# A four-layer graph kernel: LSTM input kept graph by graph, and layer 3's weights multiplied together on the chip

## The chip, the cores and the metric

The kernel runs on one core of a Trainium2 chip. The metric is the device time of one execution in microseconds (us). All data are float32.

## The reference

The input x is 128 graphs x 64 nodes x 256 features, 8192 tokens in all. Four layers each add something to x after a layernorm and a relu. Cut to what matters:

```
# layer 0: two graph convolutions, then LSTMs over windows of p = 1..4 nodes
h = relu(adj @ (h @ Wg0 + bg0)); h = relu(adj @ (h @ Wg1 + bg1))
for p in 1..4:                       # nw = 64 // p windows per graph
    wins = h[:, :nw*p].reshape(B*nw, p, 256)
    last = lstm_last(Wih[p-1], Whh[p-1], ..., wins)
    h[:, arange(nw)*p + (p-1)] = last        # the last node of each window is replaced
# layer 1: A_hat @ x, linear 256->512, batchnorm, relu, linear 512->256, batchnorm
# layer 2: three weights, with the diagonal, upper and lower part of adj, and a bias
# layer 3: causal attention inside each graph, with adj added to the scores
q, k, v = split(h @ Wqkv)
attn = softmax(where(causal, q @ k.T * scale + adj, -1e30))
y = (attn @ v) @ Wo
```

## The kernel before, in words

Tokens are handled in 16 supertiles of 512 (`NS`, `SUP`), two graphs per 128 partitions, or with features on partitions and tokens along the row (`KC` = 2 chunks of 128 features). One list of Python loops writes the program; the tile framework adds the waits and may hoist an instruction, but each engine runs its own instructions in order. Every matmul writes one of eight PSUM banks (`bank()`, all under the name `ps`). Loads of tokens and LSTM weights are issued on SP's queue, loads of constants on ScalarE's.

The stages are:

- **Layer 0, first part** (lines 206 to 232): for each supertile, layernorm, two aggregations and two linear maps. The last line, L232, applies the relu and writes the features into `hT`.
- **LSTM** (lines 235 to 307): for p = 1 to 4, weights `wih` and `whh` are loaded and the tokens are taken in blocks of up to 512 windows, two blocks at a time. `step` makes the gates: for each gate half, two products of `wih` with node j of each window, read from `hT` by `cols`, and from the second node on two of `whh` with the state `hn` (all L276), then an activation (L278). VectorE combines the gates (L285 to L294), and L298 writes the last state back into `hT`. When j = 0 the forget gate is left out, so a block has 12 products with `wih` for the first node and 16 for each later one.
- **Layer 1** (lines 324 to 379): a first pass over the supertiles makes the token-major x1 (transposes at L185), aggregates, multiplies with `w1` (L350) and gathers statistics; a second pass (L366 to L378) follows when all statistics are in.
- **Layers 2 and 3** (lines 382 to 476): for each supertile, transposes back, layernorm (L158 to L165), aggregation (L400), layer 2's products (L411), layernorm, transposes of h (L421) into `h3T` (L422), products with `wqkv` for q and k (L427, copied by ScalarE at L429), for v (L435, L438), scores (L443), softmax (L446 to L453), transposes of the weights (L456, L458), the product with v (L463, L465), with `wo` (L470), and the sum (L473), which is stored. Every supertile is written out in this order, and its steps depend on each other.

A group of `hT` holds 2048 tokens, 32 graphs. Node t of graph b lies at column t x 32 + b, so for any p and j `cols` reads runs of 32 adjacent words. Because layer 1 wants the tokens of one graph together, GpSimd copies each supertile's features into `hs` first (L341, through `graphs`). There is one group of memory more than groups of tokens (`hbuf`, the last in the pool `hlast`), since `place(s)` lets layer 1's results lie one group behind their inputs. The pool `late` takes hlast's place when layer 1's first pass is over, and only then are layer 2's and layer 3's weights loaded (L357 to L360), which the trace has at 1657.7 to 1661.2 us.

Of the kernel before, what the change touches and what calls it, by code (L numbers as in the profile page):

```python
# [20 lines left out]
def kernel(ctx: ExitStack, tc: tile.TileContext, a: dict, out: bass.AP):  # L21
# [37 lines left out]

    def load_const(name, src, shape, pool=const):  # L60
        t = pool.tile(shape, F32, tag=name, name=name)
        nc.scalar.dma_start(t, src)
        return t

    def row_bcast(name, src, n, pool=const):
        t = pool.tile([P, n], F32, tag=name, name=name)
        nc.scalar.dma_start(t, bass.AP(tensor=src.tensor, offset=src.offset, ap=[[0, P], [1, n]]))
        return t

    def weight(name, src, pool=const):  # L70
        k, m = src.shape
        return load_const(name, src.rearrange("(c p) m -> p c m", p=P), [P, k // P, m], pool)

# [24 lines left out]
    bn1 = load_const("bn1", a["bn1"], [P, 3, HC])  # L98
    bn2 = load_const("bn2", a["bn2"], [P, 3, KC])

    lbias = const.tile([P, NL, NM], F32, tag="lbias", name="lbias")
# [77 lines left out]
    def to_token_major(src, add, dst):  # L179

        for q2 in range(0, Q, 2):
# [5 lines left out]

    last = ExitStack()  # L190
    hlast = last.enter_context(tc.tile_pool(name="hlast", bufs=1, side="right"))
    hbuf = [(hpool if g < NG else hlast).tile([P, KC, GRP], F32, tag=f"hT{g}", name=f"hT{g}")
            for g in range(NG + 1)]
    hT = hbuf[1:]

    def place(s):
        return hbuf[s // SG], (s % SG) * SUP

    def graphs(s, c):

        v = hT[s // SG][:, c, :].rearrange("p (t b) -> p b t", b=GB)
        b = (s % SG) * (SUP // T)
        return v[:, b : b + SUP // T, :]


    with tc.tile_pool(name="pa", bufs=2) as pa, tc.tile_pool(name="pax", bufs=3) as pax:
        for s in range(NS):
            xt = pax.tile([P, Q, D], F32, tag="xt", name="xt")
            nc.sync.dma_start(xt, x_r[s])
            h = layernorm_relu(pa, xt)  # L210
            g0 = aggregate(pa, h, adjT_bd, "g0")
            h1 = pa.tile([P, Q, D], F32, tag="h1", name="h1")
            for q2 in range(0, Q, 2):
                p_ = bank().rearrange("p (q d) -> p q d", q=2)
                for q in range(2):
                    for c in range(KC):
                        nc.tensor.matmul(p_[:, q, :], g0[:, c, ts(q2 + q, P)], wg0[:, c, :],
                                         start=(c == 0), stop=(c == KC - 1))
                nc.vector.tensor_add(h1[:, q2 : q2 + 2, :], p_,
                                     rsb[:, None, :].to_broadcast([P, 2, D]))  # L220
            nc.scalar.activation(h1, h1, AF.Relu)
            g1 = aggregate(pa, h1, adjT_bd, "g1")
            for o in range(KC):
                p_ = bank()
                for c in range(KC):
                    nc.tensor.matmul(p_, wg1[:, c, ts(o, P)], g1[:, c, :],
                                     start=(c == 0), stop=(c == KC - 1))
                t = pa.tile([P, SUP], F32, tag="h2", name="h2")
                nc.vector.scalar_tensor_tensor(
                    t.rearrange("p (q n) -> p q n", q=Q), bcast_q(rs_row), bg1[:, o : o + 1],  # L230
                    p_.rearrange("p (q n) -> p q n", q=Q), op0=ALU.mult, op1=ALU.add)
                nc.scalar.activation(graphs(s, o), t.rearrange("p (b t) -> p b t", t=T), AF.Relu)  # L232


    with tc.tile_pool(name="lw", bufs=2) as lw, tc.tile_pool(name="lg", bufs=2) as lg, \
            tc.tile_pool(name="lh", bufs=3) as lh:
        for p in range(1, NL + 1):
# [7 lines left out]
            nw = T // p  # L245
            per = 512 // GB
            nblk = -(-nw // per)
            cut = [i * nw // nblk for i in range(nblk + 1)]
            blocks = [(g, w0, w1 - w0) for g in range(NG) for w0, w1 in zip(cut, cut[1:])]

            def cols(blk, c, j):
                g, w0, n = blk
                v = hT[g][:, c, :].rearrange("p (t b) -> p t b", b=GB)
                return v[:, w0 * p + j : (w0 + n - 1) * p + j + 1 : p, :]

            def step(blk, j, state):
                last = j == p - 1
                N = blk[2] * GB
                gate = {}
                for name, gi, fn in (("i", 0, AF.Sigmoid), ("g", 2, AF.Tanh),  # L260
# [5 lines left out]
                    for hc in range(KC):  # L266
# [5 lines left out]
                        for n, (w, r, c) in enumerate(ops):  # L272
                            o_ = p_[:, :N]
                            if n < KC:
                                o_ = o_.rearrange("p (w b) -> p w b", b=GB)
                            nc.tensor.matmul(o_, w[:, c, ts(m, P)], r,  # L276
# [19 lines left out]
                else:  # L296
                    for c in range(KC):
                        nc.vector.tensor_mul(  # L298
                            cols(blk, c, j),
                            gate["o"][:, c, :N].rearrange("p (w b) -> p w b", b=GB),  # L300
                            gate["g"][:, c, :N].rearrange("p (w b) -> p w b", b=GB))

# [21 lines left out]

    with tc.tile_pool(name="pz", bufs=1) as pz:
        zb = [pz.tile([P, HC - KC, SUP], F32, tag=f"z{s}", name=f"z{s}") for s in range(NS)]
# [7 lines left out]

        with tc.tile_pool(name="pb", bufs=2) as pb, tc.tile_pool(name="pbx", bufs=2) as pbx:
            for s in range(NS):
                xt = pbx.tile([P, Q, D], F32, tag="xt", name="xt")
                nc.sync.dma_start(xt, x_r[s])
                hs = pb.tile([P, KC, SUP], F32, tag="hs", name="hs")
                for c in range(KC):  # L340
                    nc.gpsimd.tensor_copy(hs[:, c, :].rearrange("p (b t) -> p b t", t=T), graphs(s, c))  # L341
                x1 = pbx.tile([P, Q, D], F32, tag="x1", name="x1")
                to_token_major(lambda c, q: hs[:, c, ts(q, P)], xt, x1)
                nc.sync.dma_start(x1d[s], x1)
                h = layernorm_relu(pb, x1)
                ag = aggregate(pb, h, ahT, "ag")
                for o in range(HC):
                    p_ = bank()
                    for c in range(KC):
                        nc.tensor.matmul(p_, w1[:, c, ts(o, P)], ag[:, c, :],  # L350
                                         start=(c == 0), stop=(c == KC - 1))
                    z = zslot(s, o)
                    nc.scalar.activation(z, p_, AF.Identity, bias=bn1[:, 0, o : o + 1])
                    nc.vector.bn_stats(st1[:, o, s, :], z)
        last.close()
        late = ctx.enter_context(tc.tile_pool(name="late", bufs=1, side="right"))
        wl2 = [weight(f"wl2_{k}", a["W"][k], late) for k in range(3)]  # L357
        bl2 = row_bcast("bl2", a["bias"], D, late)
        wqkv = weight("wqkv", a["Wqkv"], late)
        wo = weight("wo", a["Wo"], late)  # L360
        co1 = bn_coeffs(pz, st1, HC, bn1, "bn1")

        for s in range(NS):
# [11 lines left out]
            for o in range(KC):  # L375
                y = zslot(s, o)
                nc.vector.tensor_scalar_add(y, acc[o], bn2[:, 0, o : o + 1])
                nc.vector.bn_stats(st2[:, o, s, :], y)  # L378
        co2 = bn_coeffs(pz, st2, KC, bn2, "bn2")


    with tc.tile_pool(name="pc", bufs=2) as pc, tc.tile_pool(name="pc1", bufs=1) as pc1:
        for s in range(NS):
# [34 lines left out]
            for c in range(KC):  # L418
# [3 lines left out]
                nc.vector.tensor_copy(h3T[:, c, :], p_)  # L422
            qk = pc1.tile([P, 2 * KC, SUP], F32, tag="qk", name="qk")
            for o in range(2 * KC):
                p_ = bank()
                for c in range(KC):
                    nc.tensor.matmul(p_, wqkv[:, c, ts(o, P)], h3T[:, c, :],  # L427
                                     start=(c == 0), stop=(c == KC - 1))
                nc.scalar.copy(qk[:, o, :], p_)  # L429
            v = pc.tile([P, Q, D], F32, tag="v", name="v")  # L430
            for q2 in range(0, Q, 2):
                p_ = bank().rearrange("p (q d) -> p q d", q=2)
                for q in range(2):
                    for c in range(KC):
                        nc.tensor.matmul(p_[:, q, :], h3T[:, c, ts(q2 + q, P)],  # L435
                                         wqkv[:, c, 2 * D : 3 * D],
                                         start=(c == 0), stop=(c == KC - 1))
                nc.scalar.copy(v[:, q2 : q2 + 2, :], p_)  # L438

            p_ = bank()  # L440
            for q in range(Q):
                for c in range(KC):
                    nc.tensor.matmul(p_[:, ts(q, P)], qk[:, c, ts(q, P)], qk[:, KC + c, ts(q, P)],  # L443
                                     start=(c == 0), stop=(c == KC - 1))
# [15 lines left out]
            for c in range(KC):  # L460
                p_ = bank()
                for q in range(Q):
                    nc.tensor.matmul(p_[:, ts(q, P)], v[:, q, ts(c, P)], eT[:, ts(q, P)],  # L463
                                     start=True, stop=True)
                nc.scalar.copy(yT[:, c, :], p_)  # L465
            for q2 in range(0, Q, 2):
                p_ = bank().rearrange("p (q d) -> p q d", q=2)
                for q in range(2):
                    for c in range(KC):
                        nc.tensor.matmul(p_[:, q, :], yT[:, c, ts(q2 + q, P)], wo[:, c, :],  # L470
                                         start=(c == 0), stop=(c == KC - 1))
# [43 lines left out]
```

## Time and profile before

| | us |
|---|---|
| median of 2 runs (2765.78 to 2766.38) | 2766.08 |
| the profiled execution | 2765.78 |
| its span, first to last instruction | 2764.1 |
| layer 0, first part, until the first LSTM matmul | 243.8 |
| LSTM p = 1, 2, 3, 4 | about 168, 308, 337, 371 |
| layer 1, first and second pass | about 280 and 118 |
| layers 2 and 3 | about 936 |

PE is TensorE's matmul, PEld its weight load, DVE VectorE, ACT ScalarE, POOL GpSimd, SP the engine that issues token loads. In the profile one float32 matmul leaves two PE records. [...] the distance from one start to the next, or busy time divided by count, says what a record takes of the stream. Groups in the tables are named by line; L165 and L185 are helpers used by several stages.

### The profile page before, as it was taken

To read this page: it belongs to the slowest core of one execution; us is meant where nothing else is said; L and a number is where in the kernel's file an instruction comes from. 1 tells how busy PE (TensorE), PEld (TensorE's weight loads), DVE (VectorE), ACT (ScalarE), POOL (GpSimd) and SP (SyncE) were. 2 spreads that over 40 slices of the span, in tenths; PEclk is the share of its full clock that TensorE was granted. 3 is DMA by queue.
4 is the path that set the end of the run, shared out by engine and by line. 5 is a ranking of instruction groups with operands and counts; after the bars stand their busy time and mean duration, and the time that the engine had idled before them with its cause. 6 is when DMAs were issued, how large, how long until landed. Compare 5 with 4: busy or idle time off the path is not lost. (4 is left out here: it accounts for less than half of the span.)

```text
span 2764.1 us, 18958 instructions
## 1 busy us (share of the span) xinstructions
PE 2398.7 (87%) x7588; PEld 1419.9 (51%) x7588; DVE 778.9 (28%) x1564; ACT 787.6 (28%) x1331; POOL 139.0 (5%) x126
## 2 busy tenths in 40 slices
PE   6888999999999999999986667978778787787877
PEld 5664444444666665444444444445555555555555
DVE  5542221112222121121124443452222222222222
ACT  3333442333333233222222224302222222222221
POOL 1000000000000000000011110000010000000000
PEclk9999999999999999999998898988888888888888
DMA  3101000000000000000001111000000000000000
GB/s 110 39 16 61 0 13 3 1 0 0 31 1 0 0 0 0 0 0 0 0 15 61 61 64 56 0 23 15 16 31 16 15 16 16 31 16 16 16 8 16
DMA packets 35977, 54.29 MB, mean 20 GB/s; under 512 B 2608, under 2 KB 29488, under 8 KB 35888
## 3 DMA queue, kind: packets, MB, share of 16 engines
q1 hardware_dynamic: 31856, 49.29, 5.5%
q10 hardware_dynamic: 4032, 3.78, 0.4%
q8 instruction: 60, 0.98, 0.2%
q14 instruction: 29, 0.24, 0.0%
HBM read 36.28 MB, written 16.78 MB: 19 GB/s over the span
## 5 line engine op out<-in xcount | busy, mean ns | idle before, releaser
L276 PE MATMUL ps<-hT,wih 128*128 128x512 f32 (+2 forms) x2016 | 810.9, 542 | 7.1 <-DMA wih<-in_WihT_dram 7.1
L276 PEld LDWEIGHTS ps<-hT,wih 128*128 128x128 f32 x2016 | 383.7, 190 | 387.5 <-issue 322.4
L276 PE MATMUL ps<-hn,whh 128*128 128x512 f32 (+2 forms) x1152 | 466.2, 527 | 0.0
L276 PEld LDWEIGHTS ps<-hn,whh 128*128 128x128 f32 x1152 | 218.9, 190 | 200.4 <-issue 153.1
L165 ACT ACTIVATE ln_h<-x,ln_rn 128x256 f32<-128x256 f32 x192 | 99.6, 589 | 523.2 <-DVE ln_rn L162 523.2
L400 PE MATMUL ps<-adj,ln_h 128*128 128x384 f32 x256 | 126.5, 667 | 84.8 <-ACT ln_h L165 84.8
L411 PE MATMUL ps<-wl,ag 128*128 128x256 f32 x768 | 168.4, 379 | 0.0
L278 ACT ACTIVATE gg<-ps,lbias 128x512 f32<-128x512 f32 (+2 forms) x144 | 91.9, 638 | 231.9 <-PE ps L276 231.9
L411 PEld LDWEIGHTS ps<-wl,ag 128*128 128x128 f32 x768 | 145.9, 190 | 23.3
L278 ACT ACTIVATE gi<-ps,lbias 128x512 f32<-128x512 f32 (+2 forms) x144 | 91.8, 638 | 229.9 <-PE ps L276 229.9
L427 PE MATMUL ps<-h3T,wqkv 128*128 128x512 f32 x256 | 144.8, 730 | 9.1 <-DVE h3T L422 9.1
L288 DVE TENSOR_TENSOR gi<-gi,gg 128x1024 f32<-128x1024 f32 (+2 forms) x36 | 38.2, 1062 | 385.6 <-ACT gg L278 385.6
L400 PEld LDWEIGHTS ps<-adj,ln_h 128*128 128x128 f32 x256 | 67.1, 270 | 138.4 <-ACT ln_h L165 88.8
L175 PE MATMUL ps<-ahT,ln_h 128*128 128x128 f32 x256 | 61.0, 429 | 86.2 <-ACT ln_h L165 86.2
L278 ACT ACTIVATE go<-ps,lbias 128x512 f32<-128x512 f32 (+2 forms) x144 | 91.3, 634 | 89.1 <-PE ps L276 86.8
L350 PE MATMUL ps<-ag,w 128*128 128x512 f32 x256 | 116.6, 605 | 0.0
L161 POOL TENSOR_TENSOR ln_rn<-ln_rn,mhalf 128x4 f32<-128x4 f32 x64 | 64.8, 1012 | 987.4 <-DVE ln_rn L160 979.2
L427 PEld LDWEIGHTS ps<-h3T,wqkv 128*128 128x128 f32 x256 | 60.0, 242 | 87.1 <-issue 63.3
L341 POOL COPY hs<-hT 128x512 f32<-128x512 f32 x32 | 32.8, 1061 | 1422.0 <-DVE hT L298 1254.8
L175 PEld LDWEIGHTS ps<-ahT,ln_h 128*128 128x128 f32 x256 | 57.5, 316 | 90.0 <-ACT ln_h L165 90.0
L285 DVE TENSOR_TENSOR cell<-gi,gg 128x1024 f32<-128x1024 f32 (+2 forms) x36 | 41.2, 1144 | 210.3 <-ACT gg L278 210.3
L291 ACT ACTIVATE gg<-cell 128x1024 f32<-128x1024 f32 (+1 forms) x72 | 68.7, 954 | 82.2 <-DVE cell L290 82.2
(121 smaller groups left out, 2265.6 us busy)
## 6 DMA issues: line engine op xcount, KB each, us to landing
xt<-in_x_dram SPq DMA_DIRECT2D x32, 512.0 KB, 4.5
x1d<-x SPq DMA_DIRECT2D x16, 512.0 KB, 2.9
x<-x1d SPq DMA_DIRECT2D x16, 512.0 KB, 3.9
out_dram<-x SPq DMA_DIRECT2D x16, 512.0 KB, 3.1
wih<-in_WihT_dram SPq DMA_DIRECT2D x4, 1024.0 KB, 5.6
whh<-in_WhhT_dram SPq DMA_DIRECT2D x3, 1024.0 KB, 9.2
wl<-in_W_dram ACTq DMA_DIRECT2D x3, 256.0 KB, 5.5
wqkv<-in_Wqkv_dram ACTq DMA_DIRECT2D x1, 768.0 KB, 7.2
```

Source lines behind the costliest of these rows:

```text
L161: nc.gpsimd.tensor_tensor(rn[:, 0, :], rn[:, 0, :], mhalf[:, :Q], ALU.pow)
L165: nc.scalar.activation(h[:, q, :], src[:, q, :], AF.Relu, bias=rn[:, 1, q : q + 1], scale=rn[:, 0, q : q + 1])
L175: nc.tensor.matmul(p_[:, ts(q, P)], h[:, q, ts(c, P)], mT, start=True, stop=True)
L276: nc.tensor.matmul(o_, w[:, c, ts(m, P)], r, start=(n == 0), stop=(n == len(ops) - 1))
L278: nc.scalar.activation(gt[:, hc, :N], p_[:, :N], fn, bias=lbias[:, l, m : m + 1])
L285: nc.vector.tensor_mul(c_, i_, g_)
L288: nc.vector.tensor_mul(i_, i_, g_)
L291: nc.scalar.activation(g_, c_, AF.Tanh)
L350: nc.tensor.matmul(p_, w1[:, c, ts(o, P)], ag[:, c, :], start=(c == 0), stop=(c == KC - 1))
L400: nc.tensor.matmul(p_, h[:, q, ts(c, P)], adj3.rearrange("p k n -> p (k n)"), start=True, stop=True)
L411: nc.tensor.matmul(p_[:, q, :], ag[:, c, k, ts(q2 + q, P)], wl2[k][:, c, :], start=(n == 0), stop=(n == 3 * KC - 1))
L427: nc.tensor.matmul(p_, wqkv[:, c, ts(o, P)], h3T[:, c, :], start=(c == 0), stop=(c == KC - 1))
```

## The change

Two things are exchanged in one diff.

*The LSTM buffer.* `hT` is laid out graph by graph: node t of graph b lies at column b x 64 + t. `cols` then reads element steps of p words, in runs of one graph's windows. L232's write and layer 1's transposes use adjacent words, so `graphs`, `hs` and the GpSimd copies are gone, and so are `hlast` and `late`. The blocks are taken over graphs: `nb` graphs with all their windows, 512 columns for p = 1, 2 and 4 and 336 for p = 3 (before: 320 and 352), and as many blocks as before (16, 8, 8, 4).

*Layer 3.* Between layer 0's first part and the LSTM a new block loads Wqkv and Wo, transposes Wq, Wk and Wv, and makes wqk = Wq Wk^T and wvo = Wv Wo once. In layer 3, `h3T` takes the place of k in the scores and the layernorm's result h the place of v; `wvo` stands for `wo`.

Besides, layer 2's weights and bias are loaded with the other constants at the start, and layer 1's pool of input tiles has three buffers instead of two.

```diff
+    wl2 = [weight(f"wl2_{k}", a["W"][k]) for k in range(3)]
+    bl2 = row_bcast("bl2", a["bias"], D)
...
-        v = hT[s // SG][:, c, :].rearrange("p (t b) -> p b t", b=GB)
...
-                nc.scalar.activation(graphs(s, o), t.rearrange("p (b t) -> p b t", t=T), AF.Relu)
+                nc.scalar.activation(dst[:, o, c0 : c0 + SUP], t, AF.Relu)
+    with tc.tile_pool(name="wt", bufs=1) as wt:
+        wqkv = wt.tile([P, KC, 3 * D], F32, tag="wqkv", name="wqkv")
+        nc.scalar.dma_start(wqkv, a["Wqkv"].rearrange("(c p) m -> p c m", p=P))
+        wo = wt.tile([P, KC, D], F32, tag="wo", name="wo")
+        nc.scalar.dma_start(wo, a["Wo"].rearrange("(c p) m -> p c m", p=P))
+        wT = wt.tile([P, 3 * KC, D], F32, tag="wT", name="wT")
+        for k in range(3):
+            p_ = bank().rearrange("p (d c) -> p d c", d=KC)
+            for d in range(KC):
+                for c in range(KC):
+                    nc.tensor.transpose(p_[:, d, ts(c, P)], wqkv[:, c, ts(k * KC + d, P)], ident)
+            nc.vector.tensor_copy(wT[:, k * KC : (k + 1) * KC, :], p_)
+        for left, right, to in ((0, wT[:, KC : 2 * KC, :], wqk), (2, wo, wvo)):
+            p_ = bank().rearrange("p (c m) -> p c m", c=KC)
+            for c in range(KC):
+                for d in range(KC):
+                    nc.tensor.matmul(p_[:, c, :], wT[:, left * KC + d, ts(c, P)], right[:, d, :],
+                                     start=(d == 0), stop=(d == KC - 1))
+            nc.vector.tensor_copy(to, p_)
...
-                g, w0, n = blk
-                v = hT[g][:, c, :].rearrange("p (t b) -> p t b", b=GB)
-                return v[:, w0 * p + j : (w0 + n - 1) * p + j + 1 : p, :]
+                g, b = blk
+                v = hT[g][:, c, :].rearrange("p (b t) -> p b t", t=T)
+                return v[:, b : b + nb, j : j + (nw - 1) * p + 1 : p]
...
-                hs = pb.tile([P, KC, SUP], F32, tag="hs", name="hs")
-                for c in range(KC):
-                    nc.gpsimd.tensor_copy(hs[:, c, :].rearrange("p (b t) -> p b t", t=T), graphs(s, c))
...
-            qk = pc1.tile([P, 2 * KC, SUP], F32, tag="qk", name="qk")
-            for o in range(2 * KC):
+            qk = pc1.tile([P, KC, SUP], F32, tag="qk", name="qk")
+            for o in range(KC):
...
-                    nc.tensor.matmul(p_, wqkv[:, c, ts(o, P)], h3T[:, c, :],
+                    nc.tensor.matmul(p_, wqk[:, c, ts(o, P)], h3T[:, c, :],
...
-            v = pc.tile([P, Q, D], F32, tag="v", name="v")
-            for q2 in range(0, Q, 2):
-                p_ = bank().rearrange("p (q d) -> p q d", q=2)
...
-                    nc.tensor.matmul(p_[:, ts(q, P)], qk[:, c, ts(q, P)], qk[:, KC + c, ts(q, P)],
+                    nc.tensor.matmul(p_[:, ts(q, P)], qk[:, c, ts(q, P)], h3T[:, c, ts(q, P)],
...
-                    nc.tensor.matmul(p_[:, ts(q, P)], v[:, q, ts(c, P)], eT[:, ts(q, P)],
+                    nc.tensor.matmul(p_[:, ts(q, P)], h[:, q, ts(c, P)], eT[:, ts(q, P)],
...
-                        nc.tensor.matmul(p_[:, q, :], yT[:, c, ts(q2 + q, P)], wo[:, c, :],
+                        nc.tensor.matmul(p_[:, q, :], yT[:, c, ts(q2 + q, P)], wvo[:, c, :],
```

More of the change, by code (lines that the diff above doesn't have):

```diff
@@ L57, in bank, with load_const, row_bcast, weight @@
         return psum.tile([P, 512], F32, tag="ps", name="ps")
-    def load_const(name, src, shape, pool=const):
-        t = pool.tile(shape, F32, tag=name, name=name)
+    def load_const(name, src, shape):
+        t = const.tile(shape, F32, tag=name, name=name)
         nc.scalar.dma_start(t, src)
         return t
-    def row_bcast(name, src, n, pool=const):
-        t = pool.tile([P, n], F32, tag=name, name=name)
+    def row_bcast(name, src, n):
+        t = const.tile([P, n], F32, tag=name, name=name)
         nc.scalar.dma_start(t, bass.AP(tensor=src.tensor, offset=src.offset, ap=[[0, P], [1, n]]))
         return t
-    def weight(name, src, pool=const):
+    def weight(name, src):
         k, m = src.shape
-        return load_const(name, src.rearrange("(c p) m -> p c m", p=P), [P, k // P, m], pool)
+        return load_const(name, src.rearrange("(c p) m -> p c m", p=P), [P, k // P, m])
     ident = const.tile([P, P], F32, tag="ident", name="ident")
@@ L99 @@
     bn2 = load_const("bn2", a["bn2"], [P, 3, KC])
+    wl2 = [weight(f"wl2_{k}", a["W"][k]) for k in range(3)]
+    bl2 = row_bcast("bl2", a["bias"], D)
+    wqk = const.tile([P, KC, D], F32, tag="wqk", name="wqk")
+    wvo = const.tile([P, KC, D], F32, tag="wvo", name="wvo")
     lbias = const.tile([P, NL, NM], F32, tag="lbias", name="lbias")
@@ L186, in to_token_major @@
             nc.vector.tensor_add(dst[:, q2 : q2 + 2, :], add[:, q2 : q2 + 2, :], p_)
[L190 to L194, printed above, removed]
-    def place(s):
-        return hbuf[s // SG], (s % SG) * SUP
-    def graphs(s, c):
-        v = hT[s // SG][:, c, :].rearrange("p (t b) -> p b t", b=GB)
-        b = (s % SG) * (SUP // T)
-        return v[:, b : b + SUP // T, :]
+    hT = [hpool.tile([P, KC, GRP], F32, tag=f"hT{g}", name=f"hT{g}") for g in range(NG)]
+    def place(s):
+        return hT[s // SG], (s % SG) * SUP
     with tc.tile_pool(name="pa", bufs=2) as pa, tc.tile_pool(name="pax", bufs=3) as pax:
@@ L222 @@
             g1 = aggregate(pa, h1, adjT_bd, "g1")
+            dst, c0 = place(s)
             for o in range(KC):
@@ L245 @@
             nw = T // p
[L246 to L249, printed above, removed]
+            nb = 1
+            while 2 * nb * nw <= 512 and 2 * nb <= GB:
+                nb *= 2
+            N = nb * nw
+            blocks = [(g, b) for g in range(NG) for b in range(0, GB, nb)]
             def cols(blk, c, j):
-                g, w0, n = blk
-                v = hT[g][:, c, :].rearrange("p (t b) -> p t b", b=GB)
-                return v[:, w0 * p + j : (w0 + n - 1) * p + j + 1 : p, :]
+                g, b = blk
+                v = hT[g][:, c, :].rearrange("p (b t) -> p b t", t=T)
+                return v[:, b : b + nb, j : j + (nw - 1) * p + 1 : p]
             def step(blk, j, state):
                 last = j == p - 1
-                N = blk[2] * GB
                 gate = {}
@@ L274, in step @@
                             if n < KC:
-                                o_ = o_.rearrange("p (w b) -> p w b", b=GB)
+                                o_ = o_.rearrange("p (b t) -> p b t", b=nb)
                             nc.tensor.matmul(o_, w[:, c, ts(m, P)], r,
@@ L299, in step @@
                             cols(blk, c, j),
-                            gate["o"][:, c, :N].rearrange("p (w b) -> p w b", b=GB),
-                            gate["g"][:, c, :N].rearrange("p (w b) -> p w b", b=GB))
+                            gate["o"][:, c, :N].rearrange("p (b t) -> p b t", b=nb),
+                            gate["g"][:, c, :N].rearrange("p (b t) -> p b t", b=nb))
             for k in range(0, len(blocks), 2):
@@ L323, in bn_coeffs @@
         return co
-    with tc.tile_pool(name="pz", bufs=1) as pz:
+    with tc.tile_pool(name="pz", bufs=1) as pz, tc.tile_pool(name="pb", bufs=2) as pb, \
+            tc.tile_pool(name="pbx", bufs=3) as pbx:
         zb = [pz.tile([P, HC - KC, SUP], F32, tag=f"z{s}", name=f"z{s}") for s in range(NS)]
@@ L333, in zslot @@
             return g[:, c, c0 : c0 + SUP] if c < KC else zb[s][:, c - KC, :]
[L335 to L338, printed above, removed]
-                hs = pb.tile([P, KC, SUP], F32, tag="hs", name="hs")
-                for c in range(KC):
-                    nc.gpsimd.tensor_copy(hs[:, c, :].rearrange("p (b t) -> p b t", t=T), graphs(s, c))
[L342 to L348, printed above, removed]
-                    for c in range(KC):
[L350 to L361, printed above, removed]
+        for s in range(NS):
+            g, c0 = place(s)
+            xt = pbx.tile([P, Q, D], F32, tag="xt", name="xt")
+            nc.sync.dma_start(xt, x_r[s])
+            x1 = pbx.tile([P, Q, D], F32, tag="x1", name="x1")
+            to_token_major(lambda c, q: g[:, c, c0 + q * P : c0 + (q + 1) * P], xt, x1)
+            nc.sync.dma_start(x1d[s], x1)
+            h = layernorm_relu(pb, x1)
+            ag = aggregate(pb, h, ahT, "ag")
+            for o in range(HC):
+                p_ = bank()
+                for c in range(KC):
+                    nc.tensor.matmul(p_, w1[:, c, ts(o, P)], ag[:, c, :],
+                                     start=(c == 0), stop=(c == KC - 1))
+                z = zslot(s, o)
+                nc.scalar.activation(z, p_, AF.Identity, bias=bn1[:, 0, o : o + 1])
+                nc.vector.bn_stats(st1[:, o, s, :], z)
@@ L363 @@
+        co1 = bn_coeffs(pb, st1, HC, bn1, "bn1")
         for s in range(NS):
@@ L378 @@
                 nc.vector.bn_stats(st2[:, o, s, :], y)
-        co2 = bn_coeffs(pz, st2, KC, bn2, "bn2")
+        co2 = bn_coeffs(pb, st2, KC, bn2, "bn2")
     with tc.tile_pool(name="pc", bufs=2) as pc, tc.tile_pool(name="pc1", bufs=1) as pc1:
@@ L422 @@
                 nc.vector.tensor_copy(h3T[:, c, :], p_)
-            qk = pc1.tile([P, 2 * KC, SUP], F32, tag="qk", name="qk")
-            for o in range(2 * KC):
+            qk = pc1.tile([P, KC, SUP], F32, tag="qk", name="qk")
+            for o in range(KC):
                 p_ = bank()
                 for c in range(KC):
-                    nc.tensor.matmul(p_, wqkv[:, c, ts(o, P)], h3T[:, c, :],
+                    nc.tensor.matmul(p_, wqk[:, c, ts(o, P)], h3T[:, c, :],
                                      start=(c == 0), stop=(c == KC - 1))
                 nc.scalar.copy(qk[:, o, :], p_)
-            v = pc.tile([P, Q, D], F32, tag="v", name="v")
-            for q2 in range(0, Q, 2):
-                p_ = bank().rearrange("p (q d) -> p q d", q=2)
[L433 to L438, printed above, removed]
             p_ = bank()
```

## The prediction

> **What bounds the kernel now.** I read the busy shares first, then a table of windows cut at the stages, then the chain of waits inside one stage, then groups of single lines. The busy shares and slices:
>
> ```profile
> PE 2398.7 (87%) x7588; PEld 1419.9 (51%) x7588; DVE 778.9 (28%) x1564; ACT 787.6 (28%) x1331; POOL 139.0 (5%) x126
> ...
> PE   6888999999999999999986667978778787787877
> ```
>
> 87% is an average over stages with different limits. The windows (columns: window, its length, then busy us and count for PE, PEld, DVE, ACT, POOL, then granted clock, DMA share, GB/s) show the last LSTM pass, layer 1's two stages, and layers 2 and 3:
>
> ```profile
> 1040.00:1430.00 390.00, 387.39 (x922) 174.58 (x920) 72.94 (x65) 102.63 (x145) 1.26 (x2) 1.00 0.00 0
> 1430.00:1710.00 280.00, 189.07 (x640) 118.12 (x639) 120.86 (x296) 77.33 (x129) 48.62 (x48) 0.85 0.20 64
> 1710.00:1828.00 118.00, 112.87 (x258) 49.70 (x258) 49.07 (x73) 45.07 (x64) 0.70 (x1) 0.98 0.00 1
> 1828.00:2764.00 936.00, 724.90 (x2623) 510.37 (x2622) 245.02 (x639) 199.74 (x449) 70.01 (x48) 0.82 0.06 18
> ```
>
> The LSTM, 244 to 1428 us, is TensorE alone: busy all of it at full clock, no other engine at more than half. Time added to an LSTM matmul is added to the kernel. Layers 2 and 3 take 936 us, 58.5 per supertile (512 tokens, 16 of them), with TensorE busy 77%. That is no second resource but one dependency chain. The chain in order of time, around layer 3 (start, length, what):
>
> ```profile
> 2148.52 0.61 ACT ln_h L165
> ...
> 2149.18 1.96 PE ps L421 x7
> 2151.16 0.70 DVE h3T L422
> 2151.86 0.04 issue
> 2151.91 9.04 PE ps L427 x16
> 2160.95 3.45 PE ps L435 x16
> 2164.40 1.80 PE ps L443 x16
> 2166.22 0.70 DVE sc L446
> ```
>
> There is no step of the next supertile in it: TensorE's work and its waits are in series, so matmuls taken out here come off the end one for one, until a wait that they covered shows.
>
> [...] No TensorE read in this trace steps over words[...]. It has one such access, ScalarE's write at L232, in steps of 128 bytes (columns: group | busy us, mean ns of one | idle before it, releaser):
>
> ```profile
> L232 ACT ACTIVATE hT<-h 128x512 f32<-128x512 f32 x32 | 33.1, 1105 | 100.0 <-DVE h L229 100.0
> L221 ACT ACTIVATE h<-h 128x1024 f32<-128x1024 f32 x16 | 16.9, 1056 | 41.3 <-DVE h L219 41.3
> ```
>
> L232 takes 1105 ns for 512 columns, L221, the same Relu on adjacent words, 1056 ns for 1024. L291's widths (1051 ns at 1024, 733 at 640) put 0.83 ns on a column, so 512 adjacent ones would take 1056 - 512 x 0.83 = 631 ns. The steps cost 474 ns, 0.93 ns per element: half rate. The trace thus agrees that stepping costs, for a write, of another engine, in a larger step. [...]here the first part of L427, after the 4.0 us wait for L165, runs at 0.86 us per record and its end at 0.43.
>
> **The change part by part.**
>
> *Layer 3, on the path.* Per supertile L427 falls from 16 records to 8. (Each fp32 matmul leaves two.) L427's 9.04 us are about 5 records at 0.86 and 11 at 0.43; [...]the 8 removed run at 0.43: 3.44 us. L435's 16 records and 3.45 us go. Four ScalarE copies (two qk, two v, 586 ns each) go; they were hidden. But v's matmuls covered the copy of the last qk bank: in the new order the scores follow the second q matmul and wait for its copy. That wait is ScalarE's start, 0.24, plus 0.59, plus about 0.05: 0.9 us, as L470 shows at its like place behind L465 (4.65 us where its L435-shaped twin takes 3.62: 1.0). Net 3.44 + 3.45 - 0.9 = 6.0 us, x 16 = **-96 us**. Ends: -110 (no wait) and -75[...]. Using h itself in place of v costs nothing: the same 8 matmuls of 128 columns, and its buffer is free again long before the second next layernorm.
>
> *The products on chip, new.* They stand between layer 0's first part and the LSTM. Now the wih load is issued at 238.73 us, right after the last L232, and L276 starts at 243.77. With the new pool in the same memory: the 1 MB of Wqkv and Wo arrives about 5 us after the same point (wih's 1 MB did); 12 transposes are some 3.3 us throttled, the copy 0.9, 8 matmuls of 256 columns (16 records, 0.23 to 0.45 us) 5, the copy 0.7, and only then can wih start and take 5 again. 15 us of new serial work; ends +5 (wih lies where nothing waits) and +20. I take **+14**. On ScalarE's queue the two loads stand ahead of the LSTM's activations only, which wait for matmuls anyway.
>
> *Constants earlier.* wl2 and bl2 (four issues, about 0.45 us each, 0.9 MB) move from 1657 us, where layer 1 hid them, to the start, ahead of the first layernorm activation on ScalarE's queue. That activation waits till 14.98 for VectorE, and the queue was through at 13.2; the issues also share the engines with the first x tiles on SP's queue. **+2**, ends 0 and +6.
>
> *Layout, cheap parts.* L341's 32 copies on GpSimd go. TensorE's transposes waited for them 3.2 us in all, at the first supertile: **-2**, as the second copy's wait is partly the weights' turn. L232 becomes adjacent, hidden behind VectorE except the last one: -0.5. L298's writes become stepped on VectorE: at most 0.5 us each, beside LSTM matmuls that nothing delays. A third input buffer in layer 1 removes no wait, since no wait for xt is seen there. Together, with L341: **-3**.
>
> *Layout, the dear part.* The moving operand of L276's first products is read from hT with p words between elements, where it had runs of 32 adjacent ones; p = 1 stays adjacent. The products of h (whh) are not touched, and the column counts are the same (p = 3: 336 in place of 320 and 352). Records with wih, two per product: p = 2, 8 blocks x 28 x 2 = 448; p = 3, 8 x 44 x 2 = 704; p = 4, 4 x 60 x 2 = 480. A 512-column record takes 0.43 us of the stream, a p = 3 one 337 us / 1216 = 0.277 (its whole pass by its records). So stepped time is 193 + 195 + 206 us. TensorE takes a 4-byte element each 0.84 ns, which is ScalarE's adjacent rate, so half rate would show in full. Not shown by the trace, hence bounds: nothing, or all of it doubled, +594. I take half rate from a step of 16 bytes on, p = 4 alone: **+206** (0.93 ns x 512 x 480 = 229 by ScalarE's price).
>
> **Sum** against the profiled execution, 2765.8 us (span 2764.1 and 1.7 around it; the median is 2766.1, 0.3 higher): -96 + 14 + 2 - 3 + 206 = +123, so **2890 us**, 4.5% slower.
>
> **The rivals.**
> 1. *Stepped reads are free for TensorE* (other side). Then -83: 2683 us. For it: [...]that nothing in the trace shows a stepped read to be slow; against it: L232's half rate. It decides at p = 4: below 28 us of stepping cost the kernel is over 2% faster.
> 2. *Lines with one hit pay.* With p = 3, two of four elements stand alone in their line (offsets 0, 12, 24, 36): half of 195 besides 206, +304: 2987 us.
> 3. *Every lone word pays,* p = 2 too[...]: +594: 3277 us.
> 4. *A part-hidden cost,* a quarter to two thirds of p = 4 (+30 to +139): 2713 to 2822 us.
> That layer 3's removal gains nothing is excluded by the chain; that it does not do what it says too, for h (Wq Wk^T) h^T and (e h)(Wv Wo) are the same products in another order.
>
> **Chances.** Measurement tells some 2% (55 us) from no change. Likeliest case 0.30, rival 1 0.22, rival 2 0.22, rival 3 0.13, rival 4 0.10, others above 0.03. Range 2665 to 3010: from rival 1 with the better ends of the small terms (2765.8 - 110 + 5 - 3 = 2658, most of it) to rival 2 with most of ScalarE's price (304 x 0.93 / 0.84 = 337, 3020); it leaves out rival 3 and the rest, 0.16 to 0.2. The likeliest case alone spans 2865 to 2925. Faster by over 2%: 0.22; within 2%: 0.10; slower: 0.68.
>
> **What would show it.** In the changed trace: L276's wih records by pass. p = 4's at twice 0.43 us apart, p = 2's and p = 3's unchanged, whh's unchanged. In layers 2 and 3, 52.5 us per supertile with a new wait of the score matmuls for qk's copy. Before the first L276 a gap near 20 us in place of 7. The prediction is wrong if p = 4's records stay at 0.43 us (then rival 1), or if p = 2's grow.

## The result, and the profile after

The changed kernel takes 3022.59 us (median of 2 runs, 3019.89 to 3025.29) where the kernel before takes 2766.08: ratio 1.0927, 95% interval 1.088 to 1.0974. It is slower, as forecast, but by 256 us and not by 124, and lies 13 us above the forecast's range. The span of its profiled execution is 3023.5 us.

The first view is the table of windows, cut within 2 us of the points at which the stages begin in each trace (the columns are those of the prediction's table of windows; a cut a little late moves at most 0.6 us between rows of the table by stage). The kernel before, its LSTM passes p = 3 and p = 4, then layers 2 and 3 from the first L400:

```profile
714.50:1057.40 342.90, 342.90 (x1214) 230.33 (x1213) 69.79 (x88) 109.82 (x200) 0.00 (x0) 1.00 0.01 5
1057.40:1427.20 369.80, 369.80 (x862) 163.40 (x860) 68.70 (x60) 96.93 (x135) 0.00 (x0) 1.00 0.00 0
...
1836.50:2764.10 927.60, 723.29 (x2616) 509.19 (x2616) 237.55 (x617) 199.06 (x448) 68.92 (x47) 0.82 0.05 17
```

The changed kernel, p = 1 and 2 together, p = 3, p = 4, and layers 2 and 3:

```profile
255.40:736.30 480.90, 480.89 (x1092) 207.51 (x1093) 101.91 (x104) 173.15 (x240) 0.00 (x0) 0.99 0.03 10
736.30:1198.40 462.10, 462.10 (x1215) 235.82 (x1214) 71.62 (x88) 110.87 (x200) 0.00 (x0) 1.00 0.01 4
1198.40:1793.20 594.80, 594.80 (x863) 171.89 (x862) 71.18 (x59) 98.20 (x135) 0.00 (x0) 1.00 0.00 0
...
2204.10:3023.50 819.40, 609.64 (x2232) 430.75 (x2232) 237.85 (x618) 161.46 (x384) 68.89 (x47) 0.80 0.06 19
```

Both LSTM passes, p = 3 and p = 4, have the same count of matmul records as before (one apart, at the cut), the same granted clock of 1.00, and TensorE busy to the last microsecond; only the time is longer. So no wait has come in: the same instructions take longer. Stage by stage:

| stage | before | after | difference | forecast |
|---|---|---|---|---|
| up to the first LSTM matmul | 243.8 | 255.4 | +11.6 | +16 |
| LSTM p = 1 and 2 | 470.7 | 480.9 | +10.2 | 0 |
| LSTM p = 3 | 342.9 | 462.1 | +119.2 | 0 |
| LSTM p = 4 | 369.8 | 594.8 | +225.0 | +206 |
| layer 1, up to layer 2's first product | 409.3 | 410.9 | +1.6 | -3 |
| layers 2 and 3 | 927.6 | 819.4 | -108.2 | -96 |
| span | 2764.1 | 3023.5 | +259.4 | +123 |

Which instructions they are is seen in the timeline of TensorE (start, length, line, operands, shape, count of records in the merged row), from the changed kernel in p = 2, p = 3 and p = 4. In each pass products with `wih`, whose moving operand is read from `hT`, alternate with products with `whh`, whose operand `hn` has adjacent words:

```profile
448.19 1.96 PE L292 MATMUL ps<-hT,wih 128*128 128x512 f32 x4
449.99 1.88 PE L292 MATMUL ps<-hn,whh 128*128 128x512 f32 x4
...
759.02 1.97 PE L292 MATMUL ps<-hT,wih 128*128 128x336 f32 x4
760.82 1.30 PE L292 MATMUL ps<-hn,whh 128*128 128x336 f32 x4
761.96 1.97 PE L292 MATMUL ps<-hT,wih 128*128 128x336 f32 x4
...
1245.15 3.76 PE L292 MATMUL ps<-hT,wih 128*128 128x512 f32 x4
1248.73 1.90 PE L292 MATMUL ps<-hn,whh 128*128 128x512 f32 x4
1250.47 1.06 PE L292 MATMUL ps<-hT,wih 128*128 128x512 f32 x1
```

Read the distance from one start to the next, not the lengths, which run past the next start. In p = 4 four stepped records take 1248.73 - 1245.15 = 3.58 us, 0.895 each, and four adjacent ones 1.74, 0.435: 2.06 times. In p = 3 it is 1.80 and 1.14, 0.45 against 0.285 at 336 columns: 1.58 times. In p = 2 it is 0.45 against 0.43. So a stepped record takes the same 0.45 us with 512 columns in p = 2 as with 336 in p = 3: the count of words does not set its time.

In layer 3 the chain of waits of the changed kernel (start, length, what) shows the removed products gone and a new wait in their place:

```profile
2485.51 0.70 DVE h3T L430
...
2486.26 5.52 PE ps L435 x8
2491.80 0.59 ACT qk L437
...
2492.44 1.84 PE ps L442 x14
2494.31 0.70 DVE sc L445
```

ScalarE's copy of the second qk bank stands in the chain, where before the v products hid it. From the start of the copy of h3T to VectorE's first step on the scores are now 8.8 us (2485.51 to 2494.31), before 15.06 (2151.16 to 2166.22).

### The profile page after: what moved, and what is told of

It is laid out like the page before. It is cut to its first block, busy times and chain, and to the rows that moved or that the text cites. A ratio compares the mean times of both kernels' runs of the same rounds, so it can differ in the third digit from the quotient of the medians.

```text
span 3023.5 us, 18134 instructions
## 1 busy us (share of the span) xinstructions
PE 2649.0 (88%) x7232; PEld 1362.4 (45%) x7232; DVE 786.6 (26%) x1569; ACT 740.2 (24%) x1267; POOL 106.1 (4%) x94
## 5 line engine op out<-in xcount | busy, mean ns | idle before, releaser
L292 PE MATMUL ps<-hT,wih 128*128 128x512 f32 (+1 forms) x2016 | 1165.2, 722 | 5.1 <-DMA wih<-in_WihT_dram 5.1
L292 PE MATMUL ps<-hn,whh 128*128 128x512 f32 (+1 forms) x1152 | 469.0, 529 | 0.0
L294 ACT ACTIVATE gi<-ps,lbias 128x512 f32<-128x512 f32 (+1 forms) x144 | 91.9, 638 | 345.5 <-PE ps L292 345.5
L304 DVE TENSOR_TENSOR gi<-gi,gg 128x1024 f32<-128x1024 f32 (+1 forms) x36 | 38.2, 1062 | 520.8 <-ACT gg L294 520.8
L294 ACT ACTIVATE gg<-ps,lbias 128x512 f32<-128x512 f32 (+1 forms) x144 | 91.9, 638 | 327.1 <-PE ps L292 327.1
L294 ACT ACTIVATE go<-ps,lbias 128x512 f32<-128x512 f32 (+1 forms) x144 | 91.5, 635 | 182.6 <-PE ps L292 181.2
L301 DVE TENSOR_TENSOR cell<-gi,gg 128x1024 f32<-128x1024 f32 (+1 forms) x36 | 41.2, 1144 | 262.4 <-ACT gg L294 262.4
L294 ACT ACTIVATE gf<-ps,lbias 128x512 f32<-128x512 f32 (+1 forms) x72 | 44.8, 623 | 233.0 <-PE ps L292 233.0
L305 DVE TENSOR_TENSOR cell<-gf,cell 128x1024 f32<-128x1024 f32 (+1 forms) x36 | 38.2, 1062 | 239.6 <-ACT gf L294 239.6
L435 PE MATMUL ps<-h3T,wqk 128*128 128x512 f32 x128 | 88.6, 857 | 9.1 <-DVE h3T L430 9.1
```

What stands on the lines that cost most here:

```text
L292: nc.tensor.matmul(o_, w[:, c, ts(m, P)], r, start=(n == 0), stop=(n == len(ops) - 1))
L294: nc.scalar.activation(gt[:, hc, :N], p_[:, :N], fn, bias=lbias[:, l, m : m + 1])
L435: nc.tensor.matmul(p_, wqk[:, c, ts(o, P)], h3T[:, c, :], start=(c == 0), stop=(c == KC - 1))
```

## The experiments

### What pattern of words does TensorE read at full speed?

The prediction had bounded this cost and not measured it. The kernel `a_steps` is the changed kernel with 18 groups of products put behind the LSTM. They read one chunk `v` of `hT` in different patterns, and their results are not used:

```diff
+    p_ = bank()
+    for r in range(24):
+        nc.tensor.matmul(p_, w1[:, r % KC, ts(r % HC, P)], v[:, 0:1536:3], start=(r == 0), stop=(r == 23))
+    nc.vector.tensor_copy(sink, p_[:, :8])
```

> After the LSTM this kernel adds 18 groups of 24 matmuls (48 records each) whose moving operand is read from the same buffer in different patterns; their results go nowhere. Read is the time of one 512-column record, 0.43 us for adjacent words. Theory 1 (lines): a 16-byte line from which only one word is wanted costs 0.91 ns more. Then step 2 0.43 to 0.45, step 3 0.66, step 4 0.90, and every larger step, 5 to 64, 0.90 as well; two adjacent words of one line 0.43 wherever the next two lie; two adjacent words across a line border 0.90. Theory 2 (bytes): the stream fetches all bytes that it passes over, 8 per 0.84 ns. Then step 3 0.65, step 4 0.86, but step 8 1.7 and step 16 3.4, and two words in every eight 0.86. Theory 3 (pairs): only adjacent pairs stream fully; then step 2 is as slow as step 4, which the changed kernel already speaks against.

It ran once. The timeline has each group as one row of 48 records. Before none of them has TensorE any idle time, and full lines take 0.429 us per record in the first group (L330) and in the last but one (L394). After the LSTM's last write-back, early in the first group, no other engine touches `hT`. In order: adjacent words, steps of 2, 3, 4, 8 and 64 words; the second and third word of every four; then two adjacent words in every eight, once at offset 0 and once at offset 3:

```profile
1791.09 20.76 PE L330 MATMUL ps<-hT,w 128*128 128x512 f32 x48
1811.68 21.76 PE L334 MATMUL ps<-hT,w 128*128 128x512 f32 x48
...
1854.89 32.59 PE L342 MATMUL ps<-hT,w 128*128 128x512 f32 x48
1887.30 43.37 PE L346 MATMUL ps<-hT,w 128*128 128x512 f32 x48
...
2104.25 44.23 PE L366 MATMUL ps<-hT,w 128*128 128x512 f32 x48
...
2189.48 41.45 PE L374 MATMUL ps<-hT,w 128*128 128x512 f32 x48
...
2252.38 21.76 PE L382 MATMUL ps<-hT,w 128*128 128x512 f32 x48
2273.97 22.16 PE L386 MATMUL ps<-hT,w 128*128 128x512 f32 x48
2295.97 43.36 PE L390 MATMUL ps<-hT,w 128*128 128x512 f32 x48
```

From start to start, divided by 48, one record of 512 columns takes the times below. The last column counts lines: a line here is a unit for counting, as in theory 1, four words (16 bytes) from the start of `v` on, and is counted anew whenever the stream comes to it from another line; the patterns of 5 words and more pass over the same lines two to sixteen times.

| pattern | us per record | lines of 16 bytes per word |
|---|---|---|
| adjacent | 0.429 | 0.25 |
| step 2, even or odd start | 0.450 | 0.5 |
| step 3 | 0.675 | 0.75 |
| step 4, two starts | 0.900 | 1 |
| steps 5, 6, 7, 8 | 0.913, 0.895, 0.911, 0.918 | 1 |
| steps 16, 64 | 0.858, 0.860 | 1 |
| two words of every four, at offset 0 or 1 | 0.450 | 0.5 |
| two words of every eight, inside a line | 0.458 | 0.5 |
| two words of every eight, across a border | 0.900 | 1 |
| four words of every eight, one line or two | 0.429, 0.450 | 0.25, 0.5 |

Theory 2 (bytes) falls: at step 8 it wanted 1.7 us and at 64 far more, where 0.918 and 0.860 were measured. Theory 3 (pairs) falls at step 2, 0.450 us against 0.900 at step 4. Theory 1 (lines) fits for the most part, and more simply than it was written: the records measured here take as long as the greater of 0.84 ns for each word (0.429 us / 512) and **1.76 ns for each line** (0.900 us / 512), whether one or two words of the line are used. This meets 16 of the 18 groups within about 2%; steps of 16 and 64 words are some 5% quicker than it says, and why was not found. It is a count that fits the times; what in the hardware lies behind it, no run shows. Step 3 takes 0.75 x 512 x 1.76 ns = 0.675 us, as the row says.

The two words across a border show it best: as many adjacent words and the same step, but at offset 3 they lie in two lines and take 0.900 us, at offset 0 in one and take 0.458. A line of two words would not fit: the second and third word of every four would lie in two such lines, yet take the same 0.450 us as the first and second. Nor would one of eight words: the two words at offset 3 of every eight would lie in one, as those at offset 0 do, yet take twice as long.

The LSTM's own passes fit. The words of one graph for one node lie in all 16 lines of that graph, whether p is 2, 3 or 4. A record of p = 2 or p = 3 covers 16 graphs, so 256 lines or 0.45 us (measured 0.45), and one of p = 4 covers 32 graphs, so 512 lines or 0.90 us (measured 0.895).

### Is it the read, or something else in the layout?

`c_adjacent` keeps the layout, the blocks and the stepped write-backs, and takes the step out of the reads. Its LSTM reads the first nodes of each graph for every j, so it computes on other inputs:

```diff
+            def near(blk, c):
+                g, b = blk
+                v = hT[g][:, c, :].rearrange("p (b t) -> p b t", t=T)
+                return v[:, b : b + nb, 0:nw]
...
-                        ops = [(wih, cols(blk, c, j), c) for c in range(KC)]
+                        ops = [(wih, near(blk, c), c) for c in range(KC)]
```

> The changed kernel, but every product with wih reads the first nodes of each graph as adjacent words, for every node j: the LSTM's input is another one. Write-backs stay stepped, the blocks stay over graphs. If the stepped read is all of it, the LSTM takes 1184 us as before the change, in place of 1538, and the kernel 3022.6 - 354 = 2669 us. If the blocks over graphs or the stepped write-backs of VectorE have a share, it stays above that by the share: 20 us or more would show as waits of TensorE inside the LSTM.

One run: 2674.6 us. The groups of the LSTM's matmuls (busy us, mean ns of one, idle before), first with `wih` before the change and in the changed kernel, then both groups of this kernel:

```profile
L276 PE MATMUL ps<-hT,wih 128*128 128x512 f32 (+2 forms) x2016 | 810.9, 542 | 7.1 <-DMA wih<-in_WihT_dram 7.1
...
L292 PE MATMUL ps<-hT,wih 128*128 128x512 f32 (+1 forms) x2016 | 1165.2, 722 | 5.1 <-DMA wih<-in_WihT_dram 5.1
...
L297 PE MATMUL ps<-hT,wih 128*128 128x512 f32 (+1 forms) x2016 | 814.3, 543 | 5.1 <-DMA wih<-in_WihT_dram 5.1
L297 PE MATMUL ps<-hn,whh 128*128 128x512 f32 (+1 forms) x1152 | 466.0, 526 | 0.0
```

Of the 354 us that the products with `wih` had gained, 351 are gone, with the stepped write-backs in place, and among TensorE's waits there is none of an LSTM matmul but for the first weights. The read is the cause; all other parts of the layout together cost the LSTM about 3 us.

### Do the two halves add up?

`b_layout_only` is the changed kernel with layer 3 as it was:

```diff
-    wqk = const.tile([P, KC, D], F32, tag="wqk", name="wqk")
-    wvo = const.tile([P, KC, D], F32, tag="wvo", name="wvo")
+    wqkv = weight("wqkv", a["Wqkv"])
+    wo = weight("wo", a["Wo"])
...
-    with tc.tile_pool(name="wt", bufs=1) as wt:
```

> The changed kernel with layer 3 as before (wqkv, wo, the k and v products; no products of weights on the chip). If the parts add up, the stages of layers 2 and 3 lose their gain of 108 us and the gap before the LSTM its 11.6: 3022.6 + 108 - 12 = 3119 us. If the gain of layer 3 depends on the rest (pools, early loads of layer 2's weights), the sum misses by more than 5 us.

3123.53 us (ratio to the kernel before 1.129, interval 1.1274 to 1.1307), 4.5 above the sum. Layers 2 and 3 take 928.3 us from their first L387, as before the change (927.6). The first LSTM matmul starts at 246.6 instead of 255.4, so 8.8 us are given back here and not 11.6. The other 2.8 lie ahead of the LSTM. Here Wqkv and Wo are loaded with the constants at the start; whether that is the reason was not shown. The two halves are independent within 5 us, which is also the distance between the two runs of the changed kernel.

### The other combination

`d_both` takes only the good half: node by node, with layer 3's products. The block is put behind layer 1's first pass:

```diff
         wqkv = weight("wqkv", a["Wqkv"], late)
         wo = weight("wo", a["Wo"], late)
+        wqk = late.tile([P, KC, D], F32, tag="wqk", name="wqk")
+        wvo = late.tile([P, KC, D], F32, tag="wvo", name="wvo")
+        wT = late.tile([P, 3 * KC, D], F32, tag="wT", name="wT")
+        for k in range(3):
...
         co1 = bn_coeffs(pz, st1, HC, bn1, "bn1")
```

> The kernel before the change with layer 3's products merged, the block that makes them placed after layer 1's first pass, where TensorE waits about 5 us for the batchnorm coefficients. If the two halves of the change are independent, 2766.1 - 108 + about 2 = 2660 us. If the block stands in the way there (it waits for weights, and layer 1's second pass stands behind it on TensorE), 2675.

2657.3 us, ratio 0.9604 (0.9588 to 0.962): faster than both. The timeline of this kernel around the block, with layer 1's last first-pass product (L350) above and the first of its second pass (L389) below:

```profile
1701.35 7.22 PE L350 MATMUL ps<-ag,w 128*128 128x512 f32 x16
...
1708.41 1.47 PE L368 MATMUL ps<-ident,wqkv 128*128 128x128 f32 x12
...
1710.98 1.99 PE L374 MATMUL ps<-wT 128*128 128x256 f32 x8 [1.10 <-DVE wT L369]
...
1712.82 1.89 PE L374 MATMUL ps<-wo,wT 128*128 128x256 f32 x8
...
1713.94 1.52 ACT L382 ACTIVATE hT<-hT,bn1co 128x512 f32<-128x512 f32 x2 [4.64 <-DVE bn1co L322]
...
1714.80 1.98 PE L389 MATMUL ps<-hT,w 128*128 128x512 f32 x4
```

The block fills the wait for the batchnorm coefficients. From L350's start to L389's there are 13.45 us; in the kernel before there were 12.1 (1698.63 to 1710.71), with TensorE idle for 4.9 of them. In exchange the second pass starts faster: the first four records of L389 take 1.8 us (1714.80 to 1716.62 in its timeline), where those of L373 in the kernel before took 3.6 at a granted clock of 0.50. From L350's start to the ninth record of the second pass this kernel needs 17.0 us and the kernel before 18.0, so here the block costs nothing.

### Or keep the layout, and gather first

`f_gather` stays graph by graph, but for p = 3 and 4 GpSimd, idle in this stage, copies the stepped words into an adjacent tile before TensorE reads them:

```diff
+                xin = None
+                if p > 2:
+                    xin = lx.tile([P, KC, 512], F32, tag="xin", name="xin")
+                    for c in range(KC):
+                        nc.gpsimd.tensor_copy(xin[:, c, :N].rearrange("p (b t) -> p b t", t=nw),
+                                              cols(blk, c, j))
...
-                        ops = [(wih, cols(blk, c, j), c) for c in range(KC)]
+                        ops = [(wih, cols(blk, c, j) if xin is None else xin[:, c, :N], c) for c in range(KC)]
```

> The changed kernel, graph by graph, but for p = 3 and 4 GpSimd first copies the stepped words of each block and node into an adjacent tile (80 copies of up to 128x512, which took about 1.06 us each at L341 in the kernel before), and the products read that. If only the pattern that TensorE reads counts, p = 3 and p = 4 fall back to about 343 and 370 us, p = 2 keeps its 10 us, and the kernel takes 3022.6 - 119 - 225 = 2679 us plus a wait of 2 to 3 us for the first copies: 2681. If GpSimd's stepped reads are slow in their turn (over 5 us for a block's two copies)[...], waits of TensorE appear in the LSTM and the total is above 2700.

2680.08 us, ratio to the kernel before 0.9683 (0.9667 to 0.9699). GpSimd's groups in this kernel, and TensorE's products of p = 3 in its timeline:

```profile
L280 POOL COPY xin<-hT 128x512 f32<-128x512 f32 x32 | 40.3, 1289 | 291.5 <-PE ps L298 209.9 <-issue 81.6
L280 POOL COPY xin<-hT 128x336 f32<-128x336 f32 x48 | 36.5, 789 | 797.5 <-PE ps L298 391.4 <-DVE hT L320 325.3 <-issue 80.8
```

```profile
749.82 1.29 PE L298 MATMUL ps<-hn,whh 128*128 128x336 f32 x4
750.95 1.29 PE L298 MATMUL ps<-xin,wih 128*128 128x336 f32 x4
752.08 1.29 PE L298 MATMUL ps<-hn,whh 128*128 128x336 f32 x4
```

Both kinds of products now stand 1.13 us apart per four. The copies are 77 us of GpSimd's time, and TensorE waited 0.7 us for them in all. By TensorE's records p = 3 takes 343.5 us and p = 4 370.8, both as in the kernel before. The 23 us by which this kernel is slower than `d_both` are in the main p = 2's 10 us and the block of weight products before the LSTM.

## Why the prediction was wrong

**The bound** was right: every microsecond added to the LSTM's records was added to the kernel (354.4 us, in windows in which TensorE has no gap).

**The step that failed** is "I take half rate from a step of 16 bytes on, p = 4 alone: +206". That was the author's estimate; the trace of the kernel before had shown no such read by TensorE. It made p = 2 and p = 3 free and put a threshold where `a_steps` has none: 0.450 us at a step of 2 words, 0.675 at 3 and 0.900 at 4. So p = 3 pays too, 119 us, and p = 2 a little, 10 us for records of 0.45 us instead of 0.43. With 1.76 ns per line the three terms come out as 448 x 0.02 = 9, 704 x (0.45 - 0.283) = 118 and 480 x (0.90 - 0.43) = 226 us, 353 in all; measured are 354. p = 4 itself was rightly placed and sized a tenth too small (225 for 206): 1.76 ns per line is a little more than twice 0.84 ns per word.

**The rivals.** Rival 2 came nearest, with lines of 16 bytes and its offsets for p = 3, and gave 2987 us. Its size was short because it charged lone words only, and doubled them; the measured price, 1.76 ns, fits every line within 5%. Summed at ScalarE's full price it gave 3020 us, 3 us from the result, but the range was closed at 3010. That nearness is partly luck: its LSTM was 17 us short, and the other terms together were 12 us too dear. Rival 3, every lone word, would have made p = 2 as slow as p = 4, and does not hold: 0.45 us and 0.895. Rival 1's side, that stepped reads are free, holds for p = 2 alone, and nearly (0.45 against 0.43).

A better price was in the trace. L232's 0.93 ns per lone word, used for p = 3's half of lone words and all of p = 4's, gives 704 x 168 x 0.93 ns + 480 x 512 x 0.93 ns = 110 + 229 = 339 us. The likeliest case named it beside p = 4's term and left p = 3 at nothing. That ScalarE's price would carry over to TensorE was not known before `a_steps`.

**Layer 3**: the gain was forecast as 96 us and is 108, or 6.8 us per supertile. From L427's start to the scores' first record 6.97 us are gone (12.34 to 5.37, means over 16), near the 6.89 of the working; the slow start of four to five records, 0.85 us apart, stayed, as the working had counted it, at a granted clock of 0.55 before (2151.90 to 2156.20) and 0.56 after (2486.20 to 2490.40). The new wait for qk's copy costs 0.7 us and not 0.9: from the scores' first record to VectorE's first step on them 1.99 us became 2.70, with TensorE idle for 0.46, since the first product reads only the first qk bank and runs before the second copy is done. About 0.5 us more is gained in unchanged instructions, which the working had at nothing: from L470's start to the next transposes 4.50 us became 4.12, and the L400 products' 7.75 became 7.59. Why these are quicker was not tested.

**The block of weight products** was forecast as +14 with +2 for the earlier constants, and the first LSTM matmul is 11.6 us later. Almost all of it is the block, for layer 0's last activation ends when it did before (238.60 and 238.66). The weights land, the 12 transposes and 16 records follow, and `wih` is issued at 250.47, right after the last product. The working laid transposes, copy and products end to end (3.3, 0.9 and 5 us); in the trace they overlap and take from 243.19 to 250.38, 7.2 us. `d_both` shows that none of it was needed on the path.

**The cheap parts of the layout** were hidden as said: L225, the former L232, now takes 0.63 us with adjacent words, as the prediction had worked out, and changes nothing. VectorE's stepped write-backs of 512 columns rose from 693 to 746 ns in the mean (1.07 us in p = 4, where up to 0.5 us more were allowed) without delaying a matmul. Layer 1 gained nothing from losing the GpSimd copies (+1.6 instead of -3): its first transposes now start at once, but VectorE then waits 2.3 us for the first x tile. That load is issued at 1793.5, as the LSTM ends, where the kernel before had issued it at 7.8. The likely reason is that layer 1's input tiles now lie in memory that the LSTM holds; the prediction had not looked at it, and it was not tested.

**Three slips** in the working changed little. The pass p = 3 was taken as 337 us; by its records it is 343.5 (712.74 to 1056.26), so a record takes 0.283 us and not 0.277. "A quarter to two thirds" of 206 us begins at 52, not at the +30 of rival 4. And L232 is not the only stepped access of the kernel before: GpSimd's copies at L341 read `hT` in the same steps of 128 bytes, at 1061 ns for 512 columns.

## What to carry to other kernels

For a float32 moving operand, count the groups of four words (16 bytes) that a record goes through before choosing a layout. In `a_steps` TensorE took 0.84 ns per word or 1.76 ns per group, whichever was more: two words of each group were nearly enough (0.450 us per record against 0.429), a step of three or four words was not (0.675 and 0.900). Other data types were not tried. When the trace prices an unusual access on another engine, try that price on each pass in proportion to how much of it is so accessed, and don't put a threshold where no run shows one. If the layout that other stages want is the stepped one, an idle engine can gather the words first, as long as its copies stay ahead of the engine that sets the pace: in `f_gather` TensorE waited 0.7 us for 77 us of copies.

## What was not expected of the hardware

A record took nearly the same time at every step from 4 to 8 words (0.895 to 0.918 us), and a little less at 16 and 64 (0.858 and 0.860). Even two words per line were not quite free: 0.450 against 0.429, 5%. ScalarE's write in steps of 128 bytes cost 0.93 ns more per word than an adjacent one (1105 and 630 ns for 512 columns, L232 and L225), and TensorE's read at a step of four words (0.900 - 0.429) / 512 = 0.92 ns more. The two prices are alike on another engine and in the other direction; that they have one cause was not shown.
